# Moving a norm ahead of a sum, a pool of probabilities onto another place, steps by one place, and GpSimd transfers out of an end branch, in a graph layer with attention and experts

## The chip, the cores and the metric

The kernel runs on one core of one Trainium2 chip. The metric is the device time of one execution in microseconds (us), as the median over runs. The engines are written as the profile writes them: PE is TensorE (matrix products; PEld its weight loads), DVE is VectorE, ACT is ScalarE, POOL is GpSimd, SP is SyncE, which here only issues transfers. A "q" behind an engine is its sequencer.

## What is computed

4096 tokens of 256 features, a dense 4096 x 4096 adjacency matrix, everything in float32:

```python
f = layernorm(x)
deg = adj.sum(1) + 1
x = x + concat([f, adj @ (f @ neigh_W.T) / deg]) @ lin_W.T
x = layernorm(x)
h = rmsnorm(x) * ln1                  # 4 query heads, 2 key and value heads, 64 wide
q, k, v = rope(h @ wq.T), rope(h @ wk.T), h @ wv.T
x = x + softmax(causal(q @ k.T / 8)) @ v @ wo.T
flat = rmsnorm(x) * ln2
w = top 2 of softmax(flat @ router.T), their sum made 1      # 8 experts
out = x + sum over e of w[e] * (silu(flat @ w1[e].T) * (flat @ w3[e].T)) @ w2[e].T   # 682 hidden
```

## The kernel before

Tokens are cut into 8 blocks of 512, a block into 4 tiles of 128 (the partitions). `res[b]` holds block b of the running x in on-chip memory through the whole kernel, `qT` and `kT`, `vv` the queries, keys and values.

**Graph stage.** The two weight matrices of the neighbour path are multiplied first (`fold`, L282: `wn_sb` times `l2_sb` into `ml_sb`), so one projection of the normalized tokens gives both their share in the neighbours' sum and their own part. `scales_x(b)` makes mean and deviation of a block (DVE, then a power on POOL, L163 and L164), `normed_x(b, t)` writes a normalized tile into `f` (DVE, L172), `turned_x(b)` transposes the four tiles with eight PE transposes (L318) and copies them with ACT (L323), `features(b)` projects (PE, L385, four tiles), copies the neighbours' part into `g[b]` (ACT, L390), adds the own part to `res[b]` (DVE, L393), and between these calls `normed_x` for the next block.

`aggregate(b, steps)` multiplies row block b of the adjacency matrix with all `g[jb]`, in eight column blocks jb, by a scheme of seven half-size products in the place of eight (`PRODUCTS`, L423). The sums of adjacency quarters that it needs are made by `halve` on DVE, into two sets of buffers by turns: one lies in memory of the last block's `qT` and `kT`, the other is `more_sums`. After the seventh of fourteen pairs of products of a column block, the steps handed in are put into the program. The `aggregate` of block 0 carries the making of the features: for jb it runs `features(jb + 1)`, `turned_x(jb + 2)`, `halve(jb + 1)`, `scales_x(jb + 3)`. The later ones carry the making of queries, keys and values of the block before. At the end of an aggregate the products are put together in `rows` (for every second tile `rows_sums`, L443 to L451), divided by the degree, and added to `res` (L456).

**Attention.** `runs` is a list of (block, head pair, four key tiles) over the blocks in the order 3, 0, 4, 1, 5, 2, 6, 7. For each, `scores` multiplies on PE (L555) into one of three double banks, ACT takes the exponential into a tile `pt` (L560), DVE adds the tiles up (`totals`, L578), PE multiplies them with the values (`values`, L590). Scores are written one run ahead of values. What follows a finished block (output projection L624, residual, second norm, router, choice of experts) is a list of steps, `after(b)`, which `at(n, steps)` hands out to free places n, n+1 and so on between the runs (two places a run), not before place `max(ends[b, 1] + 1, end - 4)`. Behind the last of them stands `begin_experts`, which makes the table of expert groups and issues the first loads of rows and expert weights.

**Pools.** Memory is handed out as a stack: when the pools of the graph stage close, those of attention are put over the same addresses, in the order in which they are opened, and a first write there waits for the last use of what lay there. Before: `gw` (`g0` to `g7`, `more_sums`, `rows_sums`), `adjs` (three adjacency tiles), `gx`; then `eg`, `ex`, `sp` (nine `pt` tiles of 4 KB a partition), `ax`.

**Experts and end.** Groups of rows are gathered, run through `hidden` (L1105) and `combine` (L1150), and added to the output by indirect transfers issued from POOL (L1166). A number `left_over` is then read by every engine; where it is not 0 (never with this data), `rare_groups` works off groups left over, or `general_kernel` does everything over. This is the branch at L1915; L1990 stands for the end of the program.

What sets the order of work is the text itself: each engine executes its instructions in the order written, and waits for another engine where the data or a buffer demand it. The places that the change touches:

```python
218        tc.tile_pool(name="gw", bufs=1) as gw,
240        nc.scalar.dma_start(wn_sb, neigh_w.rearrange("(c p) o -> p c o", p=P))
349        more = gw.tile([P, 3, 2, 2 * P], F32, name="more_sums")
360            gw.tile([P, 2, 2, HC], F32, name="rows_sums"),
535        tc.tile_pool(name="sp", bufs=9) as sp,
1224            end = at(max(ends[b, 1] + 1, end - 4), after(b))
```

Of the kernel before, what the change touches and what calls it, by code (L numbers as in the profile page):

```python
# [9 lines left out]
F32 = mybir.dt.float32  # L10
I32 = mybir.dt.int32
SP = mybir.EngineType.SP
AF = mybir.ActivationFunctionType
ALU = mybir.AluOpType
# [3 lines left out]
P = 128  # L18
N = 4096
C = 256  # L20
NB = 8
# [31 lines left out]
RARE = 4  # L53
# [13 lines left out]
def fast_kernel(  # L67
# [24 lines left out]
    nc = tc.nc  # L92
# [3 lines left out]
    const = ctx.enter_context(tc.tile_pool(name="const", bufs=1))  # L96
# [6 lines left out]
        out=tri, in_=tri, pattern=[[1, P]], compare_op=ALU.is_gt, fill=0.0,  # L103
        base=0, channel_multiplier=-1,
# [112 lines left out]
    with (  # L217
        tc.tile_pool(name="gw", bufs=1) as gw,
        tc.tile_pool(name="adjs", bufs=3) as adjs,
        tc.tile_pool(name="gx", bufs=2) as gx,  # L220
        tc.tile_pool(name="g_tr", bufs=2, space=PSUM) as p_tr,
        tc.tile_pool(name="g_pj", bufs=2, space=PSUM) as p_pj,
# [14 lines left out]
        load_x(0)  # L237

        wn_sb, l2_sb = qT[4][:, :, 0:C], qT[5][:, :, 0:C]
        nc.scalar.dma_start(wn_sb, neigh_w.rearrange("(c p) o -> p c o", p=P))  # L240
        nc.sync.dma_start(l2_sb, lin_t[C : 2 * C, :].rearrange("(c p) o -> p c o", p=P))

        ml_sb = qT[6]
# [56 lines left out]
        HC = C // 2  # L300
# [37 lines left out]
        def normed_x(b, t):  # L338
            if t == 0:
                inputs[b] = gx.tile([P, TB, C], F32, tag="f", name=f"f_{b}", bufs=1)  # L340
            normed(inputs[b][:, t, :], b, t, rstd[b][:, t])

        def turned_x(b):
# [2 lines left out]

        halves_of = {}

        more = gw.tile([P, 3, 2, 2 * P], F32, name="more_sums")
        sums_at = [  # L350
            tuple(
                t.rearrange("p (k i) -> p k i", k=2)
# [4 lines left out]

        rows_at = [
            vv[NB - 1].rearrange("p (r h) c -> p r h c", r=2),
            gw.tile([P, 2, 2, HC], F32, name="rows_sums"),  # L360
        ]

        def halve(n):
# [16 lines left out]
        def features(b):  # L380
            fT = turned.pop(b)
            for t in range(TB):
                pj = p_pj.tile([P, 512], F32, tag="pj", name=f"pf_{b}_{t}")
                for c in range(2):
                    nc.tensor.matmul(  # L385
                        pj, fT[:, c, t * P : (t + 1) * P], ml_sb[:, c, :],
                        start=(c == 0), stop=(c == 1),
                    )
                i = t // 2 * 2
                nc.scalar.copy(  # L390
                    g[b][:, i : i + 2, t % 2, 0:HC], pj[:, 0:C].rearrange("p (h c) -> p h c", h=2)
                )
                nc.vector.tensor_add(res[b][:, t, :], res[b][:, t, :], pj[:, C : 2 * C])  # L393
                if b + 1 < NB:
                    normed_x(b + 1, t)
                if b == 0 and t == 1:
                    halve(0)
            part = [g[b][:, k, :, 0:HC] for k in range(7)]
            nc.vector.tensor_sub(part[T1], part[G12], part[G11])
            nc.vector.tensor_sub(part[T3], part[G22], part[G12])  # L400
            nc.vector.tensor_sub(part[T2], part[G22], part[T1])
            nc.vector.tensor_sub(part[T4], part[T2], part[G21])
# [126 lines left out]


    with (
        tc.tile_pool(name="eg", bufs=1) as eg,
        tc.tile_pool(name="ex", bufs=2) as ex,
        tc.tile_pool(name="sp", bufs=9) as sp,
        tc.tile_pool(name="ax", bufs=2) as ax,
        tc.tile_pool(name="a_sc0", bufs=1, space=PSUM) as p_sc0,
        tc.tile_pool(name="a_sc1", bufs=1, space=PSUM) as p_sc1,
# [6 lines left out]
        probs, sums, accs, ys, flats, chosen, squares, picks = ({} for _ in range(8))  # L544
# [652 lines left out]
        def at(n, steps):  # L1197

            for fs in steps:
                if fs[0] is None:  # L1200
                    fs = fs[1:]
                else:
                    while n in taken:
                        n += 1
                    taken.add(n)
                later.setdefault(n, []).extend(fs)
                n += 1
            return n
# [12 lines left out]
        end = 0  # L1221
        for b in ORDER[:-1]:

            end = at(max(ends[b, 1] + 1, end - 4), after(b))
        at(end, [[None, begin_experts]])
        at(2 * len(runs) - 2, [[lambda: prepare(0, p_ms, "ms")]])

# [50 lines left out]
@with_exitstack  # L1278
def rare_groups(
    ctx: ExitStack,  # L1280
    tc: tile.TileContext,
    ln2: bass.AP,
    w13: bass.AP,
    w2: bass.AP,
    out: bass.AP,
    lists: bass.AP,
    table: bass.AP,
    mine: bass.AP,
):
    nc = tc.nc  # L1290
    const = ctx.enter_context(tc.tile_pool(name="y_const", bufs=1))
    sb = ctx.enter_context(tc.tile_pool(name="y_sb", bufs=2))
    p_h = ctx.enter_context(tc.tile_pool(name="y_h", bufs=4, space=PSUM))
    p_y = ctx.enter_context(tc.tile_pool(name="y_y", bufs=2, space=PSUM))
    ident = const.tile([P, P], F32, name="y_ident")
    make_identity(nc, ident)
    ln2_sb = const.tile([P, 2], F32, name="y_ln2_sb")
    nc.sync.dma_start(ln2_sb, ln2)

    def entry(t, most):  # L1300
        return nc.values_load(
            t, engines=[SP], min_val=0, max_val=most,
            skip_runtime_bounds_check_because="the lists are as long as the tokens are many",
        )

    for i in range(RARE):
        at = entry(table[0:1, 0, i : i + 1], NE * REG)
        r = sb.tile([P, ROW], F32, tag="r", name=f"y_rows_{i}")
        nc.sync.dma_start(r, lists[bass.ds(at, P), :])
        e = entry(table[0:1, 1, i : i + 1], NE - 1)  # L1310
        w13_sb = sb.tile([P, 2, W13], F32, tag="w13", name=f"y_w13_{i}")
        nc.sync.dma_start(w13_sb, w13[bass.ds(e, 1)].rearrange("o p c w -> p (o c) w"))
        w2_sb = sb.tile([P, NF + 1, C], F32, tag="w2", name=f"y_w2_{i}")
        nc.sync.dma_start(w2_sb, w2[bass.ds(e, 1)].rearrange("o p k c -> p (o k) c"))
        tr = p_y.tile([P, 2, P], F32, tag="y", name=f"y_tr_{i}")
        xT = sb.tile([P, 2, P], F32, tag="xT", name=f"y_xT_{i}")
        for c in range(2):
            nc.tensor.transpose(tr[:, c, :], r[:, c * P : (c + 1) * P], ident)
            nc.scalar.activation(
                xT[:, c, :], tr[:, c, :], AF.Copy, scale=ln2_sb[:, c : c + 1]  # L1320
            )
        hT = sb.tile([P, NF + 1, P], F32, tag="hT", name=f"y_hT_{i}")

        def product(m):
            ps = p_h.tile([P, P], F32, tag="h", name=f"y_h_{i}_{m}")
            for c in range(2):
                nc.tensor.matmul(
                    ps, w13_sb[:, c, m * P : (m + 1) * P], xT[:, c, :],
                    start=(c == 0), stop=(c == 1),
                )  # L1330
            return ps

        for q in range(NF):
            h1, h3 = product(2 * q), product(2 * q + 1)
            si = sb.tile([P, P], F32, tag="si", name=f"y_si_{i}_{q}")
            nc.scalar.activation(si, h1, AF.Silu)
            nc.vector.tensor_mul(hT[:, q, :], si, h3)

        ht = product(2 * NF)
        si = sb.tile([P, P], F32, tag="si", name=f"y_si_{i}_t")  # L1340
        nc.scalar.activation(si[T0 : T0 + TAIL, :], ht[0:TAIL, :], AF.Silu)
        nc.vector.tensor_mul(
            hT[T0 : T0 + TAIL, NF, :], si[T0 : T0 + TAIL, :], ht[T0 : T0 + TAIL, :]
        )
        ps = p_y.tile([P, C], F32, tag="y", name=f"y_ye_{i}")
        for q in range(NF + 1):
            rows = slice(0, P) if q < NF else slice(T0, T0 + TAIL)
            nc.tensor.matmul(
                ps, hT[rows, q, :], w2_sb[rows, q, :], start=(q == 0), stop=(q == NF)
            )  # L1350
        pick = sb.tile([P, NE], F32, tag="pick", name=f"y_pick_{i}")
        nc.vector.tensor_mul(pick, r[:, C + 1 : ROW], mine[:, i, :])
        gt = sb.tile([P, 1], F32, tag="gt", name=f"y_gt_{i}")
        nc.vector.tensor_reduce(gt, pick, AX.X, ALU.add)

        where = bass.IndirectOffsetOnAxis(ap=r[:, C : C + 1].bitcast(I32), axis=0)
        inside = dict(bounds_check=N - 1, oob_is_err=False)
        was = sb.tile([P, C], F32, tag="was", name=f"y_was_{i}")
        nc.vector.memset(was, 0.0)
        nc.gpsimd.indirect_dma_start(  # L1360
            out=was, out_offset=None, in_=out[:, :], in_offset=where, **inside
        )
        y = sb.tile([P, C], F32, tag="y", name=f"y_y_{i}")
        nc.vector.scalar_tensor_tensor(y, ps, gt, was, op0=ALU.mult, op1=ALU.add)
        nc.gpsimd.indirect_dma_start(
            out=out[:, :], out_offset=where, in_=y, in_offset=None, **inside
        )

# [623 lines left out]
```

## Time and profile before

1638.8 us, median of 3 runs (1638.38 to 1639.15). The profiled execution took 1638.25 us, its span is 1636.5 us, the mean granted clock of TensorE 0.997 of full speed.

| stretch, us | what | PE busy | DVE busy |
|---|---|---|---|
| 0 to 21 | first loads, fold, first features | 13.0 of 21 | 10.2 |
| 21 to 139 | graph stage, row block 0 with the features | 113.8 of 118 | 72.1 |
| 139 to 544 | graph stage, row blocks 1 to 7 | 405.0 of 405 | 248.9 |
| 544 to 600 | first 56 us of attention | 52.6 of 56 | 37.3 |
| 600 to 1000 | attention | 394.3 of 400 | 325.1 |
| 1000 to 1109 | attention's end, first expert loads | 108.9 of 109 | 90.1 |
| 1109 to 1620 | experts | 511.0 of 511 | 143.8 |
| 1620 to 1637 | last scatter, branch, end | 4.8 of 17 | 1.4 |

How to read it: a stretch in which PE is busy all the time can be shortened only by less work for PE. Where PE is not, the waits tell which engine or transfer it stood for, and only the wait that ends last counts. In the lines of the profile "op out<-in" gives the operation with the names of its tiles, L the line of the kernel, and the brackets at the end the idle time of the engine before it with what ended it.

### The profile page before, as it was taken

What the parts mean: (1) busy time and instruction counts of PE and PEld (TensorE: products, weight loads), DVE (VectorE), ACT (ScalarE), POOL (GpSimd) and SP (SyncE); (2) the same over time, 40 slices, a digit from 0 to 9 for tenths busy, and PEclk for the clock granted to TensorE, in tenths of its full rate; (3) what the DMA queues carried; (4) which work ended last, traced back from release to release, by engine and by line L of the source; (5) the groups of instructions that cost most, each with busy time, mean ns of one, the idle gap of its engine ahead of it and who ended that gap; (6) DMA issues with size and microseconds to landing.
All of it is one profiled execution on the core that took longest, in us unless ns stands there. A gap on an engine that the chain in (4) does not pass through costs nothing.

```text
span 1636.5 us, 24754 instructions
## 1 busy us (share of the span) xinstructions
PE 1603.5 (98%) x9588; PEld 1157.6 (71%) x9588; DVE 928.8 (57%) x1914; ACT 457.9 (28%) x866; POOL 405.0 (25%) x604
## 2 busy tenths in 40 slices
PE   7999999999999999999999999999999999999997
PEld 5669999999999534344343434338888998999986
DVE  5647756756666578779778888793432222222221
ACT  2110000100000445555555455553211121221120
POOL 1001211111112221352434323412422222222122
PEclk9999999999999999999999999999999999999999
DMA  6224434434433000010001000066756777777765
GB/s 225 73 76 158 141 144 141 152 131 157 158 133 133 4 1 1 17 37 27 30 25 40 28 13 28 20 204 212 239 164 207 233 248 233 226 254 225 234 213 144
DMA packets 67711, 209.73 MB, mean 128 GB/s; under 512 B 14656, under 2 KB 46272, under 8 KB 53952
## 3 DMA queue, kind: packets, MB, share of 16 engines
q1 hardware_dynamic: 54320, 190.05, 33.4%
q0 software_dynamic: 12720, 17.47, 5.6%
q8 instruction: 78, 1.28, 0.3%
q10 hardware_dynamic: 544, 0.52, 0.1%
q14 instruction: 49, 0.40, 0.1%
HBM read 180.81 MB, written 31.42 MB: 130 GB/s over the span
## 4 chain that ended last, share of the span: by engine, by line
PE 88%; DVE 6%; issue 2%; ACT 2%; POOL 1%; DMA 1%; DVEq 0%; SPq 0%; ACTq 0%; POOLq 0%
PE acc L423 24%; PE h L1105 20%; PE ya L590 11%; PE sc L555 11%; PE ye_y L1150 10%; PE pf L385 3%; PE pq L184 3%; DVE sum L578 3%; PE po L624 2%; ACT pt L560 1%; PE tx L1083 1%; PE dn L603 1%; PE tr L318 1%; PE trq L212 1%; PE pq_l L184 0%
## 5 line engine op out<-in xcount | busy, mean ns | idle before, releaser
L560 ACT ACTIVATE pt<-sc 128x1024 f32<-128x1024 f32 (+3 forms) x288 | 251.8, 957 | 201.1 <-PE sc L555 162.5
L578 DVE TENSOR_TENSOR sum<-sum,pt 128x1024 f32<-128x1024 f32 (+3 forms) x258 | 294.3, 1141 | 20.4 <-POOL pt L562 0.5
L555 PE MATMUL sc<-qT_all,kT 64*128 64x512 f32 (+3 forms) x1152 | 253.3, 573 | 6.1 <-ACT pt L560 5.3
L423 PE MATMUL acc<-g,a 128*128 128x128 f32 x2048 | 255.7, 275 | 0.0
L590 PE MATMUL ya<-pt,vv 128*64 128x512 f32 (+3 forms) x1152 | 242.6, 563 | 0.0
L423 PEld LDWEIGHTS acc<-g,a 128*128 128x128 f32 x2048 | 241.8, 192 | 0.0
L1105 PE MATMUL h<-xT,qT_all 128*128 128x256 f32 (+1 forms) x1232 | 220.5, 335 | 0.0
L1112 DVE TENSOR_TENSOR hT<-si,h 128x256 f32<-128x256 f32 (+2 forms) x126 | 64.0, 508 | 261.1 <-ACT si L1111 261.1
L1105 PEld LDWEIGHTS h<-xT,qT_all 128*128 128x128 f32 x1232 | 194.2, 191 | 18.9 <-issue 1.0
L555 PEld LDWEIGHTS sc<-qT_all,kT 64*128 64x128 f32 x1152 | 104.2, 187 | 143.0 <-issue 105.1
L590 PEld LDWEIGHTS ya<-pt,vv 128*64 128x64 f32 x1152 | 76.3, 136 | 144.6 <-issue 138.7
L1166 POOL DMA_INDIRECT acc_dram<-y,rows x61 | 96.1, 1575 | 332.4 <-DVE y L1161 328.1
L1111 ACT ACTIVATE si<-h 128x256 f32<-128x256 f32 (+2 forms) x126 | 57.2, 454 | 376.3 <-PE h L1105 376.2
L1105 PE MATMUL h<-xT,res_all 128*128 128x256 f32 (+1 forms) x616 | 114.6, 342 | 0.0
L1105 PEld LDWEIGHTS h<-xT,res_all 128*128 128x128 f32 x616 | 100.3, 191 | 10.2 <-issue 0.2
L423 PE MATMUL acc<-g,more_sums 128*128 128x129 f32 (+1 forms) x768 | 101.7, 275 | 0.6 <-DVE more_sums L376 0.6
L423 PEld LDWEIGHTS acc<-g,more_sums 128*128 128x128 f32 x768 | 94.6, 192 | 7.5 <-issue 7.5
L1150 PE MATMUL ye_y<-res_all,hT 128*128 128x256 f32 x430 | 99.8, 379 | 0.0
L782 POOL DMA_INDIRECT lists<-row,slots x64 | 69.1, 1080 | 109.1 <-issue 106.5
L1150 PEld LDWEIGHTS ye_y<-res_all,hT 128*128 128x128 f32 x430 | 80.9, 190 | 10.5
L1161 DVE TENSOR_SCALAR y<-ye_y,gt 128x256 f32<-128x256 f32 x65 | 29.3, 481 | 86.1 <-PE ye_y L1150 86.0
L423 PE MATMUL acc<-g,qT_all 128*128 128x128 f32 (+1 forms) x512 | 74.0, 274 | 0.0
(231 smaller groups left out, 1716.5 us busy)
## 6 DMA issues: line engine op xcount, KB each, us to landing
a<-in_adj_dram SPq DMA_DIRECT2D x64, 1024.0 KB, 4.9
qT_all<-in_w_dram SPq DMA_DIRECT2D x28, 1408.0 KB, 8.2
res_all<-in_w_dram SPq DMA_DIRECT2D x28, 768.0 KB, 5.1
res_all<-in_w_dram SPq DMA_DIRECT2D x14, 1408.0 KB, 7.5
qT_all<-in_w_dram SPq DMA_DIRECT2D x14, 768.0 KB, 4.9
rows<-lists SPq DMA_DIRECT2D x25, 265.0 KB, 2.8
lists<-pad SPq DMA_DIRECT2D x8, 662.5 KB, 14.1
res_all<-in_x_dram SPq DMA_DIRECT2D x8, 512.0 KB, 9.4
```

The source lines that it names most:

```text
L184: nc.tensor.matmul(pj, hT[:, c, t * P : (t + 1) * P], wqkv_sb[:, c, :], start=(c == 0), stop=(c == 1),)
L423: nc.tensor.matmul(acc[t][bank][:, at : at + w], m[left][:, k, t * P : (t + 1) * P], g[jb][:, right, k, 0:w], start=(jb == 0 and k == 0 an ...
L555: nc.tensor.matmul(ps[:, j, :w], kT[sb][hd, i * P : (i + 1) * P], qT[b][hd, p, off:], start=True, stop=True,)
L560: nc.scalar.activation(pt[:, :, :w], ps[:, :, :w], AF.Exp, scale=HD ** -0.5)
L578: nc.vector.tensor_add(sums[b, p][:, :, off:], before[:, :, off:], pt[:, :, : 512 - off])
L590: nc.tensor.matmul(accs[b, p][hd, off:], vv[sb][:, i, hd], pt[:, j, : 512 - off], start=(s == 0), stop=(s == TB * b + TB - 1),)
L782: put = nc.gpsimd.indirect_dma_start(out=lists[:, :], out_offset=bass.IndirectOffsetOnAxis(ap=chosen[b][:, k, t, :], axis=0), in_=flats[b] ...
L1105: nc.tensor.matmul(ps[:, m % 2, m // 2 - q, :], w13_sb[:, c, m * P : (m + 1) * P], xT[:, c, :], start=(c == 0), stop=(c == 1),)
L1111: nc.scalar.activation(si[:, 0:both, :], ps[:, 0, 0:both, :], AF.Silu)
L1112: nc.vector.tensor_mul(hT[:, q : q + both, :], si[:, 0:both, :], ps[:, 1, 0:both, :])
L1150: nc.tensor.matmul(ps[h if last else 0][:, h, :], hT[:, q, cols] if q < NF else tail[:, cols], w2_sb[:, q, :], start=(q == 0), stop=(q == NF),
L1166: put = nc.gpsimd.indirect_dma_start(out=(acc_dram if k < NM - LAST else out)[:, :], out_offset=at, in_=y[:, h, :], in_offset=None, comput ...
```

## The change

Four edits, and one in code that does not run with this data.

1. In `features`, `normed_x(b + 1, t)` comes ahead of ACT's copy and DVE's sum, so that on DVE the norm does not stand behind a sum that waits for the projection and the copy.
2. `more_sums` and `rows_sums` get a pool of their own, `gs`, opened after `adjs`; in attention `sp` is opened first, so that the `pt` tiles lie where the features `g0` to `g5` lay, whose last readers are products on PE, where before they lay over `more_sums` and `rows_sums` too.
3. `wn_sb` is loaded from the SP queue, as its second transfer, ahead of `l2_sb`; ACT's queue keeps only the load into `ml_sb`.
4. The steps after a block come one place later (`ends[b, 1] + 2`).
5. `rare_groups` no longer gathers and scatters by indirect transfers of POOL: it keeps its results, makes masks of row numbers, and adds mask products to all 32 tiles of the output, with plain transfers from SP. The end branch is thereby free of GpSimd transfers on either side.

```diff
         tc.tile_pool(name="adjs", bufs=3) as adjs,
+        tc.tile_pool(name="gs", bufs=1) as gs,
         tc.tile_pool(name="gx", bufs=2) as gx,
...
-        nc.scalar.dma_start(wn_sb, neigh_w.rearrange("(c p) o -> p c o", p=P))
+        nc.sync.dma_start(wn_sb, neigh_w.rearrange("(c p) o -> p c o", p=P))
...
-        more = gw.tile([P, 3, 2, 2 * P], F32, name="more_sums")
+        more = gs.tile([P, 3, 2, 2 * P], F32, name="more_sums")
...
-            gw.tile([P, 2, 2, HC], F32, name="rows_sums"),
+            gs.tile([P, 2, 2, HC], F32, name="rows_sums"),
...
+                if b + 1 < NB:
+                    normed_x(b + 1, t)
                 i = t // 2 * 2
                 nc.scalar.copy(
                     g[b][:, i : i + 2, t % 2, 0:HC], pj[:, 0:C].rearrange("p (h c) -> p h c", h=2)
                 )
                 nc.vector.tensor_add(res[b][:, t, :], res[b][:, t, :], pj[:, C : 2 * C])
-                if b + 1 < NB:
-                    normed_x(b + 1, t)
...
+        tc.tile_pool(name="sp", bufs=9) as sp,
         tc.tile_pool(name="eg", bufs=1) as eg,
         tc.tile_pool(name="ex", bufs=2) as ex,
-        tc.tile_pool(name="sp", bufs=9) as sp,
...
-            end = at(max(ends[b, 1] + 1, end - 4), after(b))
+            end = at(max(ends[b, 1] + 2, end - 4), after(b))
...
-        nc.gpsimd.indirect_dma_start(
-            out=was, out_offset=None, in_=out[:, :], in_offset=where, **inside
-        )
...
-        nc.gpsimd.indirect_dma_start(
-            out=out[:, :], out_offset=where, in_=y, in_offset=None, **inside
-        )
+        y = const.tile([P, C], F32, name=f"y_y_{i}")
+        nc.vector.tensor_scalar(y, ps, gt, None, op0=ALU.mult)
+        ys.append(y)
...
+    for t in range(N // P):
+        ps = p_y.tile([P, C], F32, tag="y", name=f"y_add_{t}")
+        for i in range(RARE):
+            mask = sb.tile([P, P], F32, tag="mask", name=f"y_mask_{t}_{i}")
+            nc.vector.tensor_scalar(
+                mask, columns, numbers[i][:, t : t + 1], None, op0=ALU.is_equal
+            )
+            nc.tensor.matmul(ps, mask, ys[i], start=(i == 0), stop=(i == RARE - 1))
+        o = sb.tile([P, C], F32, tag="o", name=f"y_o_{t}")
+        nc.sync.dma_start(o, out[t * P : (t + 1) * P, :])
+        nc.vector.tensor_add(o, o, ps)
+        nc.sync.dma_start(out[t * P : (t + 1) * P, :], o)
```

More of the change, by code (lines that the diff above doesn't have):

```diff
@@ L1296, in rare_groups @@
     make_identity(nc, ident)
+    columns = const.tile([P, P], F32, name="y_columns")
+    tiles = const.tile([P, N // P], F32, name="y_tiles")
+    for t, n in ((columns, 1), (tiles, P)):
+        nc.gpsimd.iota(
+            t, pattern=[[n, t.shape[-1]]], base=0, channel_multiplier=0,
+            allow_small_or_imprecise_dtypes=True,
+        )
+    ys, numbers = [], []
     ln2_sb = const.tile([P, 2], F32, name="y_ln2_sb")
@@ L1354, in rare_groups @@
         nc.vector.tensor_reduce(gt, pick, AX.X, ALU.add)
[L1356 to L1359, printed above, removed]
-        nc.gpsimd.indirect_dma_start(
-            out=was, out_offset=None, in_=out[:, :], in_offset=where, **inside
-        )
-        y = sb.tile([P, C], F32, tag="y", name=f"y_y_{i}")
-        nc.vector.scalar_tensor_tensor(y, ps, gt, was, op0=ALU.mult, op1=ALU.add)
-        nc.gpsimd.indirect_dma_start(
-            out=out[:, :], out_offset=where, in_=y, in_offset=None, **inside
-        )
+        y = const.tile([P, C], F32, name=f"y_y_{i}")
+        nc.vector.tensor_scalar(y, ps, gt, None, op0=ALU.mult)
+        ys.append(y)
+        number = sb.tile([P, 1], F32, tag="number", name=f"y_number_{i}")
+        nc.vector.tensor_copy(number, r[:, C : C + 1].bitcast(I32))
+        at_tile = const.tile([P, N // P], F32, name=f"y_at_{i}")
+        nc.vector.tensor_scalar(at_tile, tiles, -1.0, number, op0=ALU.mult, op1=ALU.add)
+        numbers.append(at_tile)
+    for t in range(N // P):
[4 more added lines that the diff above has]
+                mask, columns, numbers[i][:, t : t + 1], None, op0=ALU.is_equal
+            )
+            nc.tensor.matmul(ps, mask, ys[i], start=(i == 0), stop=(i == RARE - 1))
[3 more added lines that the diff above has]
+        nc.sync.dma_start(out[t * P : (t + 1) * P, :], o)
 @with_exitstack
```

## The prediction

> **What bounds the kernel now.** I read the page's busy times first, then its chain, then the table of waits of the matmul engine stage by stage, and then the timeline around each wait that the change touches.
>
> ```profile
> PE 1603.5 (98%) x9588; PEld 1157.6 (71%) x9588; DVE 928.8 (57%) x1914; ACT 457.9 (28%) x866; POOL 405.0 (25%) x604
> PE 88%; DVE 6%; issue 2%; ACT 2%; POOL 1%; DMA 1%; DVEq 0%; SPq 0%; ACTq 0%; POOLq 0%
> ```
>
> The first line is the page's section 1: TensorE (PE) is busy 98% of 1636.5 us and no other engine more than 57%. The second is the chain that ended last: 88% PE, and what is not PE is a handful of stretches. The change removes no matmul, so it can win only where PE waits (some 33 us in all, start and tail included), or lose by adding waits. The waits of PE, first for 0 to 544 us (graph stage), then for 544 to 1110 (attention):
>
> ```profile
> PE pm L282 <- DMA qT_all<-in_lin_t_dram: 6.8, 1, 6.8
> PE tr L318 <- DVE f L172: 4.4, 8, 0.7
> PE acc L423 <- DVE more_sums L376: 0.6, 1, 0.6
> ...
> PE sc L555 <- ACT pt L560: 5.3, 4, 3.3
> ```
>
> Columns: total us, times, longest. Four places stand out: 6.8 us for the first load, eight waits of a transpose for a normalized tile, and score matmuls waiting for the exponential once for 3.3 us. From 1109 to 1620 PE is busy 511.00 of 511 us, so no gain is to be had there; 139 to 544 is 405.00 of 405. In block 0 (timeline: start, us, engine, line, in brackets the idle time before):
>
> ```profile
> 29.65 0.37 ACT L390 COPY g<-pf 128x256 f32<-128x256 f32 x1 [1.34 <-PE pf L385]
> 30.06 0.42 DVE L393 TENSOR_TENSOR res_all<-res_all,pf 128x256 f32<-128x256 f32 x1 [0.97 <-ACT g L390]
> ...
> 31.37 0.37 ACT L390 COPY g<-pf 128x256 f32<-128x256 f32 x1 [1.34 <-PE pf L385]
> 31.77 0.42 DVE L393 TENSOR_TENSOR res_all<-res_all,pf 128x256 f32<-128x256 f32 x1 [0.97 <-ACT g L390]
> 32.11 0.41 DVE L172 TENSOR_SCALAR f<-res_all,mv,rstd 128x256 f32<-128x256 f32 x1
> 32.58 0.44 PE L318 MATMUL tr<-ident,f 128*128 128x128 f32 x2 [0.59 <-DVE f L172]
> ```
>
> The norm of the last tile (L172) stands behind the sum (L393), which waits for the copy (L390), which waits for the projection: 31.33 (projection ends) + 0.37 + 0.42 + 0.41 and the hand-overs give 32.57, when the last two transposes can start. At the step into attention:
>
> ```profile
> 544.25 2.85 PE L555 MATMUL sc<-qT_all,kT 64*128 64x512 f32 x12
> 548.25 0.88 DVE L456 SCALAR_TENSOR_TENSOR res_all<-rows_sums,deg,res_all 128x256 f32<-128x256 f32 x2
> 549.36 2.85 ACT L560 ACTIVATE pt<-sc 128x1024 f32<-128x1024 f32 x3 [5.18 <-DVE res_all L456]
> 550.44 6.19 PE L555 MATMUL sc<-qT_all,kT 64*128 64x512 f32 x20 [3.34 <-ACT pt L560]
> 556.56 3.65 PE L590 MATMUL ya<-pt,vv 128*64 128x512 f32 x16
> ```
>
> PE fills the three score banks (547.1), then stands, because the first exponential waits until 549.36 for the last read of `rows_sums` (L456), over whose memory its output `pt` lies. The granted clock of the 2.6 us after that gap is 0.50, of the next 3.5 us 0.89, so the gap costs more than its own 3.3 us. The tail, after PE's end at 1624.8 (one line's instructions: duration min/median/max in ns, first and last start):
>
> ```profile
> L1915 POOLq EVENT_SEMAPHORE  x5: 17/43/2114, 1629.2 to 1631.6; - x5
> L1915 POOLq INC_SWDGE_SEM  x1: 925/925/925, 1631.7 to 1631.7; - x1
> L1990 POOLq DRAIN  x3: 46/107/3056, 1632.6 to 1636.2; - x3
> ```
>
> GpSimd waits in the end branch for its last scatter (landed about 1631.5), raises semaphores for 0.93 us, then drains for 3.06 us; the end at 1636.5 hangs on that.
>
> **What the Trainium skill says.** *Perfetto Trace Analysis*, Optimization Strategy: look for the gaps of the most contended engine in its regime and for the semaphore behind each. The trace agrees: the four gaps above are what there is. *TensorE: Matmul & The Clock Gate*, Part 1: after about one idle window of some 3.4 us the array's clock halves. Our gap of 3.34 us shows 0.50 after it. *Perfetto Trace Analysis*, DMA Instruction — SWDGE (GPSIMD): the reported end of a GpSimd transfer is that of descriptor generation, not of the data. Agrees: L1166's last instruction starts at 1627.54 and takes 1.57 us, but its data land 3.9 us after issue. *DMA: Bandwidth & Descriptors*, Issuing engines are not separate DMA queues: issuing from another engine saves only the issue time (0.45 to 0.55 us here).
>
> **Norm ahead of the sum.** In each of seven calls of `features` with a next block, `normed_x` now stands ahead of the sum. The norm reads `res[b+1]`, not `res[b]`, and depends on nothing of this tile. It runs right after the sum of the tile before it: for the last tile at about 30.5, ready at 30.9, against PE's need at about 31.8. So all eight transposes follow each other; undisturbed, in the later blocks, eight take 0.87 us (145.88 to 146.75). Now 31.17 to 32.85 is 1.68 us, so 0.8 us a column block: six times 0.80 is 4.8; at `features(0)`, where the waits are 0.69 and 0.21 and the first norms are late, I take 0.54. Sum 5.3. A lower reading is the waits themselves, 4.4; range 4.2 to 5.6. The sum (L393) comes later by at most a norm (0.41 us), and hardly that, since it had to wait for ACT. Behind it on DVE are the four sums for T1 to T4, then `halve`, whose S4 (L376) would be ready about 35.9 against 36.96 needed: hidden. DVE is busy 72 of 118 us here.
>
> **Pools.** `more_sums` and `rows_sums` move to `gs`, behind the three adjacency tiles; the `pt` tiles (nine of 4 KB a partition) go to the bottom, where `g0` to `g5` lay. As built, the first exponential then waits only for its scores (PE) and for work over before 542, the second for DVE work at 535.7, the third for 544.6 (L453). So the first starts when its scores are there, at about 545.2, done at 546.1, and PE never waits. Eight score tiles from 544.25 at 0.907 us (16 matmuls take 3.63 in the steady part) end at 551.5, against 556.6: 5.1 us. If ACT sets the pace (0.945 a tile) or half clock appears somewhere, 4; range 3.9 to 5.6. Would DVE take it back? Its own work ends only 2 us earlier (the last L456 at 549.1 stays), but its next piece that PE needs, `h_l` for the transposes at 563.78, is done at 560.2 and would come at about 558.1 against 558.75 needed; and DVE idles 5.5 us before 573.5. No table load stands there.
>
> **First load.** `wn` is now the second transfer of the SP queue, `l2` the third. Now `wn` (ACT) is issued at 0.80 and lands 4.5 us later, `l2` issued at 1.30, landing at 6.7; PE starts at 6.83. One issue (0.5 us) lies ahead of `l2` afterwards, but the other weight load (256 KB, ACT) starts 0.5 earlier and out of the way. The 16 engines share it all, so I take a loss of 0.3 us, range 0.6 loss to 0.5 gain.
>
> **Steps one place on.** As built only block 6's steps move by one half step (about 3.6 us), and with them `begin_experts`. At block 6's projection (1015 and 1020) DVE waits 0.7 and 2.4 us for PE and PE for nothing: 0, ±0.5, and up to 1 either way. `begin_experts` loads rows at 1080 and weights at 1081, first needed at 1106: over 20 us of slack hides it.
>
> **End branch.** The branch is not taken. Without GpSimd transfers in it, its other side holds no waits and no INC_SWDGE_SEM: GpSimd drains from 1629.3 instead of 1632.6. How long is not shown by the trace: 0.93 + 3.06 = 3.98 us is about one landing (3.9), so I read the drain as waiting for that instruction's own transfer. Then it would end with the last scatter or after 3.06 us, by 1632.4, SP goes on at 1632.2, and with 0.85 us of barrier the end is 1633.2: 3.3 us. If the 3.06 us start only after the scatter has landed, about 0.9 is left; at best 3.8. The larger `rare_groups` is code not run.
>
> **Sum.** 5.3 + 5.1 + 3.3 − 0.3 = 13.4; 1638.8 − 13.4 = 1625.4 us.
>
> **Rivals.** *The gains come only in part:* the drain is fixed (0.9) or DVE, over 80% busy in attention, turns the 5.1 into its own 2.1. For it: in attention's windows of 100 us between 600 and 1000 DVE is busy 79 to 84 us, PE 97 to 99.8, with waits of PE for DVE at L624 (3.1 us in all); against: DVE idles soon after the transition, as said. 13.4 − 2.4 − 3.0 gives 8, about 1630.8 with both, 1628 with one. *No change:* gains of 10 us ahead of 1109 vanish into waits for DVE and GpSimd in attention and only the 0.9 of the tail and 1 us of the rest stay: about 1637. Against: PE's waits listed there total 8.4 us now, 5.3 of them at the transition itself, so DVE seldom holds PE up. *Slower:* the moved block 6 steps stall PE for a half step (3.6 us), table and rows come late, the first load loses 0.6, and the transposes now wait for late statistics (POOL's power takes 1.0 to 2.1 us): with the gains gone 1638.8 + 3.6 + 0.6 = 1643. Against: the slack of 20 us at the experts, and statistics that are ready at 39.7 where the norm of that column block ran at 41.8 and its transposes come some 3 us later still.
>
> **From cases to numbers.** My forecast 0.70; in part 0.20; no change 0.05; slower 0.05. The range takes the ends of the unknown costs: all low, 4.2 + 3.9 + 0.9 − 0.6 − 0.5 = 7.9, gives 1630.9; all high, 16, gives 1622.8. I give 1622.5 to 1631.5, which takes in the partial case. Chances: faster 0.93, the same 0.03, slower 0.04.
>
> **What would show it.** Right: no wait of L318 on L172 left; the first L560 at about 545.2, L590 about 5 us earlier relative to the last L423, no clock under 0.9 there; no INC_SWDGE_SEM, and the end about 8.5 us after PE's end instead of 11.7. Wrong: new waits of L318 on L385's or L164's results, L555 still waiting for L560 with L456 named, a drain that ends 4 us after the scatter's landing, or PE gaps after 1000 us.

## The result and the profile after

The changed kernel takes 1625.45 us (median of 6 runs, 1624.99 to 1626.75), the kernel before 1638.59 us (6 runs, 1637.91 to 1640.32): a ratio of 0.992, 95% interval 0.9907 to 0.9933, so 13.1 us less. The predicted time was 1625.4 us. That the total fits so well is in part luck, as the sections below show: three terms were right in size, the end branch and the late place were off by about half a microsecond each, and two of the reasons given (why the first probability tile waited, what the drain at the end waits for) were wrong.

First the page of the changed kernel: sections 1 (busy times) and 4 (chain).

```profile
span 1623.3 us, 24752 instructions
PE 1600.2 (99%) x9588; PEld 1156.7 (71%) x9588; DVE 930.4 (57%) x1914; ACT 457.1 (28%) x866; POOL 402.6 (25%) x604
PE 91%; DVE 5%; ACT 2%; issue 1%; DMA 0%; POOL 0%; SPq 0%; DVEq 0%; POOLq 0%; ACTq 0%
```

PE's busy time is almost the same (1603.5 before), and the rest of the span has shrunk from 33.0 to 23.1 us. The other 3.3 us are PE work that took less time, at a higher clock or without a break in it.

The table of waits of PE, for 0 to 540 us and then for 536 to 1105 us (total, times, longest):

```profile
PE pm L283 <- DMA qT_all<-in_lin_t_dram: 7.1, 1, 7.1
PE acc L424 <- DVE more_sums L377: 0.6, 1, 0.6
PE pf L386 <- ACT qT_all L324: 0.2, 1, 0.2
PE tr L319 <- DVE f L172: 0.2, 1, 0.2
...
PE sc L556 <- ACT pt L561: 2.2, 4, 0.6
```

The eight waits for a normalized tile (4.4 us) are one of 0.2, the long wait for the exponential (3.3) is gone, and the wait for the first load is 0.3 longer. In the timeline of block 0 (start, duration, in brackets the idle time before) the norm (L172) that is shown is that of the last tile, and the sum of that tile is the second L396:

```profile
29.24 0.42 DVE L396 TENSOR_TENSOR res_all<-res_all,pf 128x256 f32<-128x256 f32 x1 [0.97 <-ACT g L393]
29.57 0.41 DVE L172 TENSOR_SCALAR f<-res_all,mv,rstd 128x256 f32<-128x256 f32 x1
30.35 1.04 PE L319 MATMUL tr<-ident,f 128*128 128x128 f32 x8
...
30.95 0.42 DVE L396 TENSOR_TENSOR res_all<-res_all,pf 128x256 f32<-128x256 f32 x1 [0.97 <-ACT g L393]
...
31.22 0.61 PE L424 MATMUL acc<-g,qT_all 128*128 128x129 f32 x4
```

The last norm is done at 29.98, before PE has ended its projection, so eight transposes run as one group and the products follow 0.87 us after their start; before it was 1.68 (31.17 to 32.85). At the step into attention:

```profile
538.66 7.14 PE L556 MATMUL sc<-qT_all,kT 64*128 64x512 f32 x32
539.92 7.44 ACT L561 ACTIVATE pt<-sc 128x1024 f32<-128x1024 f32 x8 [1.33 <-PE sc L556]
542.67 0.88 DVE L457 SCALAR_TENSOR_TENSOR res_all<-rows_sums,deg,res_all 128x256 f32<-128x256 f32 x2
545.73 1.51 PE L591 MATMUL ya<-pt,vv 128*64 128x512 f32 x6
```

The exponential starts at 539.92, 2.75 us before the last reads of `rows_sums` (L457) begin; eight tiles of scores run in one go (the granted clock is 1.00 from 538.7 to 545.7), and the values start 7.07 us after the first score in the place of 12.31. At the end (first the branch, then the end of the program; duration min/median/max in ns, first and last start):

```profile
L1934 POOLq EVENT_SEMAPHORE  x1: 17/17/17, 1618.9 to 1618.9; - x1
...
L2009 POOLq DRAIN  x3: 46/107/3397, 1619.0 to 1622.9; - x3
```

INC_SWDGE_SEM is gone, and the drain starts 1.9 us after the start of the last scatter (1617.06) where it started 5.1 us after it.

Laid along the span, the 13.2 us between the two profiles are (each a difference of two start times in the two traces):

| stretch | before | after | less, us |
|---|---|---|---|
| start to the first projection L385 | 11.98 | 11.82 | 0.16 |
| to the first product of the aggregate | 9.19 | 8.53 | 0.66 |
| to the first scores | 523.08 | 518.31 | 4.77 |
| to the first values | 12.31 | 7.07 | 5.24 |
| to the first transpose of the experts (L1083) | 549.54 | 550.10 | −0.56 |
| to the last products of PE (tail, L1150) | 518.15 | 518.15 | 0.00 |
| to the last scatter | 3.29 | 3.08 | 0.21 |
| to the end | 8.96 | 6.24 | 2.72 |

### The profile page after: what moved, and what is told of

The parts are those of the page before. It is cut to its first block, busy times and chain, and to the rows that moved or that the text cites. A ratio compares the mean times of both kernels' runs of the same rounds, so it can differ in the third digit from the quotient of the medians.

```text
span 1623.3 us, 24752 instructions
## 1 busy us (share of the span) xinstructions
PE 1600.2 (99%) x9588; PEld 1156.7 (71%) x9588; DVE 930.4 (57%) x1914; ACT 457.1 (28%) x866; POOL 402.6 (25%) x604
## 4 chain that ended last, share of the span: by engine, by line
PE 91%; DVE 5%; ACT 2%; issue 1%; DMA 0%; POOL 0%; SPq 0%; DVEq 0%; POOLq 0%; ACTq 0%
PE acc L424 24%; PE h L1106 20%; PE ya L591 12%; PE sc L556 11%; PE ye_y L1151 10%; PE pf L386 3%; DVE sum L579 3%; PE pq L184 3%; PE po L625 2%; ACT pt L561 1%; PE tx L1084 1%; PE dn L604 1%; PE tr L319 1%; DVE rden L609 1%; PE trq L212 1%
```

## The experiments

Each edit was run alone on the kernel before where that tells something, then the doubtful terms one by one. Ratios are to runs of the kernel before on the same chip, whose medians lie between 1638.75 and 1639.48 us.

**The norm alone.** `e1_norm_only`:

```diff
+                if b + 1 < NB:
+                    normed_x(b + 1, t)
                 i = t // 2 * 2
...
-                if b + 1 < NB:
-                    normed_x(b + 1, t)
```

> Before with the norm ahead of copy and sum in features, nothing else. Theory of the prediction: six column blocks lose 0.8 us of waiting each and features(0) some 0.65, so the graph stage ends 5.3 to 5.7 us earlier and the kernel takes 5.3 to 5.7 us less (about 1633.1 for 1638.6). Rival: the gain of the graph stage is taken up again in attention, where DVE has the late sums before it: graph stage 5.5 us earlier, the whole kernel at most 2 us less.

Measured 1631.85 us, ratio 0.9956 (0.994 to 0.9973); the span is 1631.2, 5.3 us under that of before. PE's waits from 0 to 540 us:

```profile
PE pm L282 <- DMA qT_all<-in_lin_t_dram: 7.0, 1, 7.0
PE acc L423 <- DVE more_sums L376: 0.6, 1, 0.6
PE tr L318 <- DVE f L172: 0.2, 1, 0.2
```

By the medians it is 6.9 us less; the interval spans 4.4 to 9.8, so the traces must tell the size. The first scores come at 539.37 in the place of 544.25 (4.88 less) and the first transpose of the experts at 1101.19 in the place of 1106.10 (4.91 less). Nothing that was won in the graph stage is given back in attention; the rival falls.

**The order of attention's pools alone.** `e2_sp_only`:

```diff
     with (
+        tc.tile_pool(name="sp", bufs=9) as sp,
         tc.tile_pool(name="eg", bufs=1) as eg,
         tc.tile_pool(name="ex", bufs=2) as ex,
-        tc.tile_pool(name="sp", bufs=9) as sp,
```

> Before with the pool of the probabilities opened first, more_sums and rows_sums left in gw. The first probability tile then lies over g0, away from rows_sums. Theory by address (the prediction's words: it waits because it lies over rows_sums): the first exponential starts at the scores' end, 5.1 us are saved. Rival, by pool: a tile waits for the last use of the whole pool over which it lies, so it still waits for L456, the last read of rows_sums; the gap stays at 3.3 us, and the kernel at 1638.6 within 0.5.

Measured 1638.47 us, ratio 0.9999 (0.999 to 1.0007). The timeline:

```profile
544.40 2.85 PE L555 MATMUL sc<-qT_all,kT 64*128 64x512 f32 x12
548.39 0.88 DVE L456 SCALAR_TENSOR_TENSOR res_all<-rows_sums,deg,res_all 128x256 f32<-128x256 f32 x2
549.39 2.85 ACT L560 ACTIVATE pt<-sc 128x1024 f32<-128x1024 f32 x3 [5.06 <-DVE res_all L456]
550.47 6.26 PE L555 MATMUL sc<-qT_all,kT 64*128 64x512 f32 x20 [3.22 <-ACT pt L560]
```

In the program as built the first probability tile now lies over `g0`, 64000 bytes a partition below `rows_sums`, and still waits for L456. Being put over other memory does not help.

**The pool of the late sums alone.** `e3_gs_only`:

```diff
         tc.tile_pool(name="adjs", bufs=3) as adjs,
+        tc.tile_pool(name="gs", bufs=1) as gs,
...
-        more = gw.tile([P, 3, 2, 2 * P], F32, name="more_sums")
+        more = gs.tile([P, 3, 2, 2 * P], F32, name="more_sums")
...
-            gw.tile([P, 2, 2, HC], F32, name="rows_sums"),
+            gs.tile([P, 2, 2, HC], F32, name="rows_sums"),
```

> Before with more_sums and rows_sums in a pool of their own behind adjs, the order of attention's pools left. The first probability tile lies over g4 and g5 as before. Theory by address: nothing of its place changes, no gain (1638.6). Rival, by pool: gw no longer holds rows_sums, so the first exponential waits for its scores alone; 5.1 to 5.3 us are saved (1633.4).

Measured 1633.79 us, ratio 0.9968 (0.9957 to 0.998). The timeline:

```profile
544.53 7.17 PE L556 MATMUL sc<-qT_all,kT 64*128 64x512 f32 x32
545.83 7.44 ACT L561 ACTIVATE pt<-sc 128x1024 f32<-128x1024 f32 x8 [1.38 <-PE sc L556]
548.53 0.88 DVE L457 SCALAR_TENSOR_TENSOR res_all<-rows_sums,deg,res_all 128x256 f32<-128x256 f32 x2
551.64 1.94 PE L591 MATMUL ya<-pt,vv 128*64 128x512 f32 x8
```

From the first score to the first values it takes 7.11 us, as in the changed kernel (7.07), though the first probability tile lies over `g4` and `g5`, exactly where it lay before (as built, it was the third tile, not the first, that lay over `rows_sums`). So what counts in this program is the pool: a tile laid over a pool that was closed waits for the last use of any tile of it, and `gw` was in use until L456 because `rows_sums` was in it. The whole gain of edit 2 is `gs`; the new order of `sp` brings nothing alone, and nothing measurable with it.

**The end branch alone.** `e4_branch_only` has the new `rare_groups` and nothing else (the diff is the last part of that of the change).

> Before with the new rare_groups alone (not run with this data). The prediction: no INC_SWDGE_SEM, the drain of GpSimd starts about 3.3 us earlier, the end comes 2.7 to 3.3 us earlier, nothing else moves (about 1635.6). Rival: the drain is a fixed 3.06 us after the last scatter has landed, then 0.9 us less (1637.7).

Measured 1635.69 us, ratio 0.9982 (0.9975 to 0.9989). From the last scatter to the end it takes 5.94 us (1627.86 to 1633.8) in the place of 8.96. Its drain:

```profile
L2008 POOLq DRAIN  x3: 46/107/3121, 1629.8 to 1633.5; - x3
```

**What the drain waits for.** The prediction read the 3.06 us as waiting for a transfer of its own. `e8_after_delay` puts GpSimd work behind the last scatter of the changed kernel, over statistics that nobody reads any more:

```diff
         combine(NM - 1)
+        for _ in range(4):
+            nc.gpsimd.tensor_tensor(rstd[0], rstd[0], half, op=ALU.pow)
     kv_scope.close()
```

> The changed kernel with four powers of one small tile on GpSimd (some 1.0 us each, 4.2 in all, over statistics no longer used) behind the last scatter, so that its drain at the end starts only after the scatter has landed. If the drain waits for GpSimd's own transfers, it is then short (under 0.5 us) and the end comes 1 to 1.5 us later than in the changed kernel. Rival: the drain takes a fixed 3.1 to 3.4 us, and the end comes 4.2 us later.

Measured 1632.35 us, one run. The timeline of GpSimd,

```profile
1618.37 1.57 POOL L1167 DMA_INDIRECT out_dram<-y,rows  x1 [0.19 <-issue]
1619.38 4.91 POOL L1275 TENSOR_TENSOR rstd<-rstd,half 128x4 f32<-128x4 f32 x4
```

and among the instructions at the end of the program (min/median/max in ns, first and last start):

```profile
L2011 POOLq DRAIN  x3: 46/107/3056, 1626.7 to 1630.3; - x3
```

The drain starts 8.3 us after the last scatter, which has long landed by then (3.7 us from issue to landing is the median of such transfers at the end of the kernel before), and takes 3056 ns as in the kernel before, to the nanosecond. My reading falls: the 3.06 us are a lower bound that hangs on no transfer. The end comes 6.0 us later than in the changed kernel (12.27 us after the last scatter's start in the place of 6.24), more than either forecast, because the drain starts 6.4 us later: the four powers take 4.9 us where 4.2 were expected, and the profile has GpSimd's next instruction only some 2.3 us after they end.

Where the scatter is still under way when the drain starts, the drain is the same or a little longer: 3121 ns in `e4_branch_only`, 3397 in the changed kernel, but 3056 again in two kernels that follow below, `e10_loads_plus1` (its scatter starts at 1615.94, its drain 2.06 us later) and `e11_loads_warm`. The first of the two:

```profile
L2009 POOLq DRAIN  x3: 46/107/3056, 1618.0 to 1621.6; - x3
```

In the seven profiles in which the drain starts 1.8 to 2.1 us after the last scatter, it ends 5.1 to 5.3 us after that scatter's start, whatever its length. So the drain seems to end at the later of two times, 3.06 us after its own start or 5.1 to 5.3 us after the start of the scatter. That the second is the landing is likely, but was not tried.

**One place later alone.** `e5_step_only` and, as its counterpart, the changed kernel with the old place, `e7_after_plus1`:

```diff
-            end = at(max(ends[b, 1] + 1, end - 4), after(b))
+            end = at(max(ends[b, 1] + 2, end - 4), after(b))
```

> Before with the steps after a block one place later, nothing else. The prediction: neutral within 0.5 us, since block 6's steps have no wait of PE before them and begin_experts has 20 us of slack. Rival, from the changed kernel's trace (between the denominator product of block 7 and the first expert transpose 43.8 us in the place of 43.3, with an exponential that starts 1.1 us late): the moved work leaves DVE behind with its sums just then, so 0.5 us are lost there, and nowhere else.

> The changed kernel with the steps back at their old place. If the late place costs 0.5 us near the end of attention, this one is 0.5 us faster than the changed kernel: 1624.9, from the denominator product of block 7 to the first expert transpose 43.3 us. Rival: the 0.5 us come from another edit, and stay (1625.4, 43.8 us).

Measured 1640.54 us, ratio 1.0005 (0.9997 to 1.0014), and 1626.16 us, ratio 0.9915 (0.9899 to 0.9932): the second was expected at 1624.9 and came out no faster than the changed kernel (1625.45), but runs that spread over 1 to 2.6 us cannot tell half a microsecond. The traces can. From the first values to the first transpose of the experts the kernels with the old place take 549.5 to 549.7 us in every profile (before, `e1_norm_only`, `e3_gs_only`, `e7_after_plus1` and others); those with the new place take 550.10 (changed kernel), 550.22 (`e5_step_only`) and 550.36 (`e8_after_delay`), but 549.55 in a second profile of the changed kernel (`e9_after_again`). Here is where it is lost, in the timeline of the changed kernel and then in its second profile:

```profile
1060.18 2.85 PE L556 MATMUL sc<-qT_all,kT 64*128 64x512 f32 x12
1062.20 3.77 ACT L561 ACTIVATE pt<-sc 128x1024 f32<-128x1024 f32 x4 [4.29 <-PE sc L556]
1063.28 1.13 PE L556 MATMUL sc<-qT_all,kT 64*128 64x512 f32 x4 [0.25 <-ACT pt L561]
```

```profile
1061.45 3.71 PE L556 MATMUL sc<-qT_all,kT 64*128 64x512 f32 x16
1062.62 1.02 ACT L561 ACTIVATE pt<-sc 128x1024 f32<-128x1024 f32 x1 [3.44 <-PE sc L556]
```

Ahead of these exponentials ACT is idle for 4.29 us, though the first scores had been ready for most of a microsecond; in the other profile it is idle for 3.44. The rival of the expectation named DVE, but DVE's sums stand alike against PE in both profiles (they start 2.59 us ahead of those scores). The break is at the same scores in `e5_step_only` and `e8_after_delay` (ACT idle for 4.38 and 4.33 us), and in none of the ten profiles with the old place. So half a microsecond is lost in three profiles of four with the late place; by what mechanism stays open.

**The first load alone.** `e6_wn_only`:

```diff
-        nc.scalar.dma_start(wn_sb, neigh_w.rearrange("(c p) o -> p c o", p=P))
+        nc.sync.dma_start(wn_sb, neigh_w.rearrange("(c p) o -> p c o", p=P))
```

> Before with the load of wn on the SP queue, nothing else. The prediction: the first product starts 0.3 us later (7.1 in the place of 6.83), the kernel takes 0.3 us more. Rival: the later start is made good before the first projection (the changed kernel has it at 11.8 against 12.0), because the transposes wait for normalized tiles too, so no difference.

Measured 1639.76 us, ratio 0.9999 (0.9991 to 1.0008). The first product starts at 7.51. Over all profiles with `wn` on SP (this one, the changed kernel twice, `e7_after_plus1`, `e8_after_delay`) it starts at 7.12 to 7.58, mean 7.44; with the old load (before and `e1_norm_only` to `e5_step_only`) at 6.82 to 7.00, mean 6.90. The edit delays the first product by 0.54 us. What of it reaches the end cannot be resolved, because what follows varies more.

**A better start, and the clock.** From the first product to the first aggregate product, the profiles without the norm's edit take either 13.7 or 14.4 us, those with it 13.2 or 14.2: two groups each. I took the clock of TensorE for the reason, and the instructions agree: in the four profiles of the shorter groups (the changed kernel, `e4_branch_only`, `e5_step_only`, `e8_after_delay`) the last product of `fold` takes 380 to 471 ns and the transposes behind it 272 or 273, in the others all products but the first take about 634 and the first transposes 421. Three kernels follow, and the changed kernel once more as a yardstick (`e9_after_again`; the last of the three ran on its own). `e10_loads_plus1`, against the changed kernel:

```diff
-        nc.sync.dma_start(wn_sb, neigh_w.rearrange("(c p) o -> p c o", p=P))
+        nc.scalar.dma_start(wn_sb, neigh_w.rearrange("(c p) o -> p c o", p=P))
         nc.sync.dma_start(l2_sb, lin_t[C : 2 * C, :].rearrange("(c p) o -> p c o", p=P))
...
-        nc.scalar.dma_start(
+        nc.sync.dma_start(
             ml_sb[:, :, C : 2 * C], lin_t[0:C, :].rearrange("(c p) o -> p c o", p=P)
...
-            end = at(max(ends[b, 1] + 2, end - 4), after(b))
+            end = at(max(ends[b, 1] + 1, end - 4), after(b))
```

`e11_loads_warm` adds to it, with 8 transposes, and `e12_loads_warm20` with 20:

```diff
+        warm = p_tr.tile([P, 2, 2, P], F32, tag="tr", name="warm")
+        for _ in range(8):
+            nc.tensor.transpose(warm[:, 0, 0, :], ident, ident)
         load_x(0)
```

> The changed kernel itself, as the yardstick for the two that follow: 0.992 of before.

> The changed kernel with wn alone on ACT's queue, the load into ml_sb on SP behind l2, and the steps at their old place. If what competes ahead of l2 sets the start, PE's first product comes at 6.5 in the place of 7.1 to 7.5 us; with 0.5 us back at the end of attention it is 0.9 to 1.2 us faster than the changed kernel. Rival: the start of the features hangs on normalized tiles and the clock, so only the 0.5 us show.

> The same with eight transposes of the identity matrix on PE ahead of everything, into a tile that nobody reads, to have TensorE's clock up when the first weights arrive. If the spread from first product to first aggregate product (13.2 or 14.2 us from run to run) comes from the clock, it is 13.2 or less here in the profile, and the kernel another 0.5 us faster on average. Rival: the spread has another cause and stays; no difference to the kernel without the transposes.

> As the kernel with eight transposes ahead, but twenty of them (0.25 us each), from 1.4 to about 6.4 us, so that PE stands for no more than 0.2 us before the first weights instead of 3.1. If the runs fall into two groups (1623.7 and 1625.7) because of TensorE's clock at the start, all runs of this kernel lie together at 1623.5 or less and the first product to the first aggregate product takes 12.7 us or less. Rival: the groups come from elsewhere; the two groups stay, with a median near 1624.5.

| kernel | median us (5 runs) | ratio to before (95%) | first product | to the aggregate |
|---|---|---|---|---|
| changed, again | 1625.09 (1625.0 to 1626.18) | 0.9916 (0.9902 to 0.9929) | 7.58 | 14.12 |
| other loads, old place | 1624.08 (1623.71 to 1625.77) | 0.9913 (0.99 to 0.9927) | 6.52 | 13.37 |
| and 8 transposes | 1625.0 (1623.73 to 1625.7) | 0.9914 (0.9901 to 0.9928) | 6.52 | 13.00 |
| and 20 transposes | 1624.17 (1623.53 to 1624.99) | 0.9911 (0.9898 to 0.9925) | 6.78 | 12.70 |

The loads do what was expected: the first product a microsecond earlier. The clock is shown by the products of `fold` themselves: those instructions (min/median/max in ns) in the kernel with other loads, then the timeline of the kernel with 20 transposes, and the same instructions there:

```profile
L283 PE MATMUL pm<-qT_all x8: 608/634/766, 6.5 to 9.6; 128*128 128x256 f32 x8
```

```profile
6.78 1.97 PE L286 MATMUL pm<-qT_all 128*128 128x256 f32 x8 [0.83 <-DMA qT_all<-in_lin_t_dram]
9.52 1.40 PE L322 MATMUL tr<-ident,f 128*128 128x128 f32 x8 [0.78 <-DVE f L172]
```

```profile
L286 PE MATMUL pm<-qT_all x8: 379/379/454, 6.8 to 8.4; 128*128 128x256 f32 x8
```

After twenty transposes, whose last starts at 5.5, a product of `fold` takes 379 ns in the place of 634, and the eight are done in 1.97 us in the place of 3.73. After eight transposes (the last starts at 2.97, and PE then stands until 6.52) the products still take 634, and reach 380 only with the last one. But with the twenty the transposes of x wait 0.78 us for the normalized tiles, which hang on the load of x and on GpSimd's power, so little of the 1.8 us is left: 12.70 in the place of 13.0 to 13.4. In time, no kernel of the three is told apart from the changed one: all intervals overlap. The forecasts of times failed: the five runs with 8 transposes still spread from 1623.73 to 1625.7, and those with 20, all expected at 1623.5 or less, from 1623.53 to 1624.99. The spans of the three profiles, 1621.9 to 1622.4, lie a microsecond under those of the changed kernel (1623.3 and 1624.5); a version that beats it beyond doubt is not shown.

## Why the prediction was right, point by point

- **Norm ahead of the sum, 5.3 us.** 4.77 in the loop and 0.66 in `features(0)`: 5.4 in the profile of the changed kernel. The second part varies: from the first projection to the first product of the aggregate it is 9.18 or 9.19 us in every profile without the edit, and with it 8.53 in five and 8.84 to 8.93 in three, `e1_norm_only` among them; so the term is 5.0 to 5.5. In the loop it is six times 0.80 as worked out; the reading by the waits alone (4.4) would have been too low: cut in two, six transposes take 0.82 us and two another 0.27, where eight together take 0.87. Shown by `e1_norm_only`.
- **Pools, 5.1 us.** 5.24, and 7.11 us from score to value with `gs` alone. The size and the wait named were right. The reason given was wrong: the first tile did not lie over `rows_sums`, but over `g4` and `g5`, and it waited because they were of one pool (`e2_sp_only`, `e3_gs_only`). The prediction had the two edits' sum from the waits of the program as built, and so came out right without knowing which of them did it.
- **DVE does not take it back.** Right: from the first values to the experts' start `e1_norm_only` and `e3_gs_only` take 549.5 us like the kernel before, and the changed kernel loses only the half microsecond of the late place.
- **First load, 0.3 us lost.** Measured 0.54 us at the first product. In the one profile of the changed kernel it was even won back (0.16 us to the good at the first projection), which is the clock of that run and not the edit (its transposes take 272 ns from the first one on, in the profile of before the first two 421): over the other profiles the first projection starts at 11.3 to 12.3 us with the old load and at 12.1 to 12.9 with the new one.
- **Steps one place on, 0.** The failed step is that slack of 20 us at the loads means no cost: the loss is not at the loads but at the scores of 1060 us, 0.5 to 0.8 us in three profiles of four.
- **End branch, 3.3 us.** 2.72 from the scatter to the end, 3.02 in `e4_branch_only`; 0.21 us in the profiles is a scatter that happened to start earlier (2.9 to 3.8 us after PE's last products, from profile to profile). The 0.3 us between the two are the longer drain of the changed kernel (3397 ns against 3121). The step that failed is that the drain waits for INC_SWDGE_SEM's own transfer. It takes at least 3.06 us without any; the gain comes because it no longer stands behind the landing (2.1 us of waiting) and behind INC_SWDGE_SEM (0.93 us), but runs beside the landing. The rival bound of 0.9 us took it as fixed and as starting only after the landing; the second half of that was wrong.

5.43 + 5.24 + 2.72 + 0.21 (scatter) + 0.16 (start) − 0.56 is 13.20, where the forecast was 5.3 + 5.1 + 3.3 − 0.3 = 13.4: an end branch mis-sized by 0.6 and a late place by 0.6 were hidden in good part by chance, at the start (0.2 won in the place of 0.3 lost) and at the scatter (0.2). By the medians the edits alone (norm, `gs`, branch, late place, load) give 6.9 + 5.0 + 3.1 − 1.1 − 0.3 = 13.6, against 13.1 for all together, which their noise allows.

As to the Trainium skill, *Perfetto Trace Analysis*, Optimization Strategy, sends the reader to the gaps of the most contended engine. That held at the two gaps of PE that the change closed: 4.4 us of waits for normalized tiles were worth 5.0 to 5.5, the 3.34 us at the step into attention 5.24. The first load's gap was named too, but the change did not shorten it, and the end of the program is no gap of PE. *TensorE: Matmul & The Clock Gate*, Part 1, has the clock halve after an idle window of about 3.4 us. The runs agree in direction, and show that the price varies: with the same gap of some 3.3 us, it is 12.25 to 12.39 us from score to value in four profiles and 13.64 or 13.65 in two, `e4_branch_only` and `e5_step_only`. In the four, eight score products after the gap take about 1057 ns in the place of 589; in the two, fourteen do. Without the gap it is 7.07 to 7.11 in all, so the edit is worth 5.2 or 6.6 us from run to run. What decides between the two is not shown.

## What to carry to other kernels

When a first write waits for something that has nothing to do with its data, look at which pool its memory belonged to before and who uses that pool last: one small late tile in a pool of large early ones holds up the whole of it, and a pool of its own frees it at once. Work that does not depend on a wait belongs ahead of it on its engine, even where the waiting engine is idle half the time. And when a sum of predicted terms hits the total, check the terms: here two errors of half a microsecond were nearly cancelled by smaller ones of the other sign, in part chance.

## What the runs showed of the hardware

- GpSimd's drain at the end of this program takes at least 3056 ns: in `e8_after_delay`, where it starts 8.3 us after the last scatter, and in `e10_loads_plus1` and `e11_loads_warm`, where it starts 2.0 or 2.1 us after it. It can lie beside the landing if nothing ahead of it in GpSimd's queue waits for that.
- A conditional with GpSimd transfers on the side that is not run cost 3.0 us on the side that is (8.96 against 5.94 us from the last scatter to the end): GpSimd waited there for the landing of the last scatter (2114 ns) and ran one INC_SWDGE_SEM of 925 ns, ahead of the drain.
- Twenty float32 transposes of 128 x 128, on nobody's input, are enough to make the products of 128 x 256 behind them fall from 634 to 379 ns. I read this as TensorE's clock: at the step into attention, where the granted clock of the profile does read 0.50, score products lengthen in the same manner, from 589 to 1057 ns. At the start the granted clock in the profile's windows is 1.00 in both kernels, so there the durations tell the clock, not that column.
